# Turning the tie rule of a list scheduler round once all groups of work are under way, in a four-layer graph network kernel

## Chip, cores and metric

The kernel runs on one core of a Trainium2 chip. The metric is the device time of one execution in microseconds (us). Engines are called PE (TensorE), ACT (ScalarE), DVE (VectorE), POOL (GpSimd) and SP (SyncE, which here only starts transfers).

## What is computed

128 graphs of 128 nodes with 128 features each go through four pre-norm attention layers. With `h = relu(layernorm(x))` ahead of each layer and `x = x + layer(h)` after it, the layers are, per graph:

```
layer 0: D[i,j] = |h[i]-h[j]|;  s = leaky(batchnorm(D @ W1.T)) @ W2;  A = softmax(masked s)
         y = leaky(batchnorm(A @ h @ Wg.T + bg));  out = [h, y] @ Wt.T + bt
layer 1: 8-head graph attention (leaky(f1[i]+f2[j]), masked softmax), elu, one more single head, elu
layer 2: single-head graph attention, elu
layer 3: 8 bilinear edge types, score chosen by the edge's type, softmax, value and output projections
```

The two batch norms of layer 0 run over all 128 graphs, so nothing after them can begin before the last graph has been seen.

## The kernel before

The program falls into three stages. **Stage A** builds the pairwise differences of every graph, multiplies them with W1 and gathers their mean and variance (`nodes` and `pairs`, with four `block`s to a graph; 160 pieces of work). **Stage B** normalises them, forms the scores, the softmax and y (`graph_scores`, `score_table`, `edges`, `attention`, then `y_norm`, `edge_types` and `first_inputs`; 179 pieces of work). **Stage C** does the rest of layer 0 and layers 1 to 3 for four graphs at a time (`group`, 32 of them, numbered 0 to 31 here). Stage C exists twice in the program, for adjacency values of only 0 and 1 and for any; a branch on `types` picks one, and with these inputs the first runs.

Within a stage no order of instructions is written out. Each piece of work is a generator that yields steps: an engine, a planned duration, the buffers that the step takes and those that it frees; a `fork` starts a side chain (a head, an edge type), and a `join` waits for it. The function `in_order` (line 54) plays all generators that are under way against each other on a planned clock. At each turn it works out for every chain when its next step could begin: not before its engine is free, its input is ready and its buffers are to be had. It emits the step that could begin first. What it emits is the program order of each engine, which nothing reorders afterwards (`manual_schedule`). At most `most` pieces of work are under way at a time: 6 in stage A, 10 in stage B, 6 in stage C. When one ends, the next begins.

Many chains usually wait for one busy engine, and then they could all begin at the same moment, when that engine comes free. So the order among equals decides much of the schedule. It is `(begin, c["age"], k)` in line 132: first the earliest beginning, then the age (the number of the piece of work; side chains have their parent's), then the place in the list. A lower age is an older piece of work. Apart from that, some buffers are kept for the oldest piece under way (`kept`): in stage C one PSUM bank `ps`, six tiles `t`, three tiles `w` and one `v`.

Steps of a group in stage C that are named below, with their lines:

- `yl` (L1136, L425), `po` of the first layer (L1142, L1145) and its sum `x` (L1150)
- the layer norm: statistics (L929, L931, L933) on DVE, `rs` (L936) on POOL, `nb` (L939) on DVE, `h` (L943) on ACT, the transposes `pt` (L951) on PE, their copy `hTc` (L954) on ACT
- `pv` (L1165) and `pf` (L1174), the values and the attention vectors of the eight heads, and `f1d` (L1195)
- the heads: `z` (L1069, L959) on PE, `p` and `q` (L1078, L1079) on ACT, `p` (L963) on DVE, `pa` (L1092) on PE, `xh` (L1098, L1099) on DVE; four such steps to a group
- after the heads: `xc` (L1214, L1216), `ptx` (L1221), `xcT` (L1224), `ph` (L1234)
- two single heads: `z` (L1243 or L1269, L1271), exponentials (L974 or L971), `po` (L1007), `ri`, `xh` (L1014, L1016), `ex` (L986), `xo` (L997, L990)
- layer 3: `pd` (L1290), `pv` (L1311), `pp` (L1104), `tt` (L1107), `ps` (L1111), the choice (L1318), exponentials (L1321, L1322), `p` (L1324), `po` (L1007), the sum `x` (L1336) and its store (L1337)

PSUM in stage C is four banks of `ps` and two double banks of `pz`; the heads' `z`, `ptx`, `ph` and `po` all take `pz`.

In stage B a score table is made of eight graphs: their score matmuls (L699), `us` (L718) on DVE, four transfers out (L728) and one in (L739) on POOL's queue, `u` (L781) on POOL, and then two `attention`s: `pl` (L788, L790, L791), `mx` and `e` (L796, L798), `pt` (L810), `py` (L817), `yt` (L820), and the store of `y` (L822). `edges` makes `negm` (L754) and `pz` (L762).

Of the kernel before, what the change touches and what calls it, by code (L numbers as in the profile page):

```python
# [51 lines left out]


def in_order(makers, most, room, kept):

    free_at = dict.fromkeys(AFTER, 0.0)
    slots = {kind: [0.0] * n for kind, n in room.items()}
    chains, events = [], {}
    started = under_way = 0
    now = 0.0

    def step(c, at):

        nonlocal under_way
        c["ready"] = at  # L70
        while True:
            said = next(c["gen"], None)
            if said is None:
                chains.remove(c)
                up = c["parent"]
                if up is None:
                    under_way -= 1
                    return
                up["open"] -= 1
                up["last"] = max(up["last"], at)  # L80
                if up["joins"] and not up["open"]:
                    up["joins"] = False
                    step(up, max(up["ready"], up["last"]))
                return
            if said[0] == "fork":
                c["open"] += 1
                step(chain(said[1], c), at)
            elif said[0] == "join":
                if c["open"]:
                    c["joins"] = True  # L90
                    return
            elif said[0] == "free":
                for kind in said[1].split():
                    slots[kind].append(at)
            elif said[0] == "wait":
                c["ready"] = at = at + said[1]
            elif said[0] == "done":
                events[said[1]] = at
            elif said[0] == "after":
                c["after"] = said[1]  # L100
            else:
                c["next"] = said
                return

    def chain(gen, parent):
        c = {"gen": gen, "parent": parent, "age": parent["age"] if parent else started, "open": 0,
             "last": 0.0, "joins": False, "next": None, "ready": 0.0, "after": None}
        chains.append(c)
        return c

    while started < len(makers) or chains:
        while started < len(makers) and under_way < most:
            under_way += 1
            c = chain(makers[started](), None)
            started += 1
            step(c, now)
        best = None
        oldest = min(c["age"] for c in chains)
        for k, c in enumerate(chains):
            if c["next"] is None or (c["after"] is not None and c["after"] not in events):  # L120
                continue
            engine, _, takes, _ = c["next"]
            begin = max(free_at[engine], c["ready"], events.get(c["after"], 0.0))
            takes = takes.split()
            for kind in set(takes):
                spare = 0 if c["age"] == oldest else kept.get(kind, 0)
                at = sorted(slots[kind])
                m = takes.count(kind)
                begin = max(begin, at[m - 1]) if len(at) >= m + spare else None
                if begin is None:  # L130
                    break
            if begin is not None and (best is None or (begin, c["age"], k) < best[0]):
                best = (begin, c["age"], k), c
        (now, _, _), c = best
        engine, work, takes, frees = c["next"]
        for kind in takes.split():
            slots[kind].remove(min(slots[kind]))
        free_at[engine] = now + work
        end = now + work + AFTER[engine]
        for kind in frees.split():  # L140
            slots[kind].append(end)
        c["next"] = c["after"] = None
        step(c, end)
# [16 lines left out]
def kernel(ctx: ExitStack, tc: tile.TileContext, x, adj, w, out):  # L160
# [269 lines left out]
    with tc.tile_pool(name="h_pool", bufs=1) as h_pool, tc.tile_pool(name="pairs", bufs=B_V) as b_v:  # L430
# [10 lines left out]
        with tc.tile_pool(name="a2", bufs=2) as a2, tc.tile_pool(  # L441
# [148 lines left out]
            with tc.manual_schedule(engines=ORDERED):  # L590
                in_order(makers, A_UNDER_WAY, {"d": A_D, "ph": 3, "v": B_V} | two, A_KEPT)
# [32 lines left out]
        with tc.tile_pool(name="b2", bufs=2) as b2p, tc.tile_pool(name="b_s", bufs=2, space=PSUM) as b_s, tc.tile_pool(  # L624
# [256 lines left out]
            with tc.manual_schedule(engines=ORDERED):  # L881
                in_order(
                    makers, B_UNDER_WAY, {"v": B_V - KEEP, "r": B_R, "pb": 6, "u": 4} | two, {"pb": 2}
                )
# [5 lines left out]
    def layers(simple):  # L890

        with tc.tile_pool(name="c_in", bufs=3) as c_in, tc.tile_pool(
# [231 lines left out]
            def group(g):  # L1124
# [213 lines left out]

            load(1)
            in_order(  # L1340
                [partial(group, g) for g in range(NB // GC)], UNDER_WAY,
                {"ps": 4, "pz": 2, "t": C_T, "w": C_W, "vals": C_V, "f": C_V, "v": C_O, "mask": C_M},
# [46 lines left out]
```

## Times and profile before

| what | us |
|---|---|
| three runs | 3172.33, 3160.60, 3168.47 |
| their median | 3168.47 |
| the profiled execution | 3172.22 |
| its span in the trace | 3170.4 |
| stage A, until its last statistics (L581, L521) | 0 to about 1248.4 |
| stage B, until `y_bi` (L417) | about 1248.5 to 2059.9 |
| stage C | 2060.0 to 3170.4 |
| of it, from the last group's `yl` on | 2975.7 to 3170.4 |

| engine | busy us | share of the span |
|---|---|---|
| PE | 2876.5 | 91% |
| DVE | 2655.7 | 84% |
| ACT | 2627.2 | 83% |
| POOL | 1494.6 | 47% |

The page cuts the span into 40 slices and shows for each the busy tenths of each engine and the clock that PE was granted (`PEclk`, in tenths of full speed). The trace gives the same for any window, and, for any window, each engine's instructions in order of time with the idle time ahead of each and what ended it.

### The profile page before, as it was taken

To read this page: it belongs to the slowest core of one execution; us is meant where nothing else is said; L and a number is where in the kernel's file an instruction comes from. 1 tells how busy PE (TensorE), PEld (TensorE's weight loads), DVE (VectorE), ACT (ScalarE), POOL (GpSimd) and SP (SyncE) were. 2 spreads that over 40 slices of the span, in tenths; PEclk is the share of its full clock that TensorE was granted. 3 is DMA by queue.
4 is the path that set the end of the run, shared out by engine and by line. 5 is a ranking of instruction groups with operands and counts; after the bars stand their busy time and mean duration, and the time that the engine had idled before them with its cause. 6 is when DMAs were issued, how large, how long until landed. Compare 5 with 4: busy or idle time off the path is not lost. (4 is left out here: it accounts for less than half of the span.)

```text
span 3170.4 us, 47435 instructions
## 1 busy us (share of the span) xinstructions
PE 2876.5 (91%) x17577; PEld 1601.7 (51%) x17577; DVE 2655.7 (84%) x4730; ACT 2627.2 (83%) x3050; POOL 1494.6 (47%) x953
## 2 busy tenths in 40 slices
PE   6999999999999998878888888689999999999996
PEld 3444433433343443233333333377787777877774
DVE  6999999999999999768777686577878878888864
ACT  4999999999999998878788787467878778877774
POOL 5999999999999996011111111122222122212211
PEclk9999999999999999989999898889999999999997
DMA  3555555555655551999999999321111111111000
GB/s 118 238 237 247 238 244 224 241 234 224 250 227 234 243 219 37 415 405 382 404 404 392 392 393 394 124 67 31 47 34 43 43 34 34 54 31 41 11 11 12
DMA packets 150723, 606.53 MB, mean 191 GB/s; under 512 B 15634, under 2 KB 99027, under 8 KB 119763
## 3 DMA queue, kind: packets, MB, share of 16 engines
q1 hardware_dynamic: 140242, 569.86, 45.6%
q0 software_dynamic: 10240, 33.53, 2.9%
q8 instruction: 143, 2.34, 0.3%
q14 instruction: 98, 0.79, 0.1%
HBM read 322.74 MB, written 280.61 MB: 190 GB/s over the span
## 5 line engine op out<-in xcount | busy, mean ns | idle before, releaser
L549 POOL TENSOR_TENSOR d<-he 128x2016 f32<-128x2016 f32 (+1 forms) x288 | 1021.6, 3572 | 63.9 <-PE ph L566 59.4
L566 PE MATMUL ph<-d,w1T 128*64 128x512 f32 (+1 forms) x4096 | 927.2, 595 | 34.6 <-DVE d L546 16.9
L552 ACT ACTIVATE d<-d 128x2016 f32<-128x2016 f32 (+1 forms) x352 | 676.7, 1926 | 13.3 <-POOL d L549 13.2
L581 DVE BATCH_NORM_STATS2 six<-v 128x6 f32<-128x512 f32 (+1 forms) x1024 | 624.0, 669 | 4.4 <-ACT v L576 4.3
L566 PEld LDWEIGHTS ph<-d,w1T 128*64 128x64 f32 x4096 | 308.0, 136 | 543.9 <-issue 397.3
L576 ACT COPY v<-ph 128x1024 f32<-128x1024 f32 (+1 forms) x512 | 510.9, 1032 | 28.9 <-PE ph L566 25.9
L546 DVE TENSOR_TENSOR d<-he,pt 128x2048 f32<-128x2048 f32 (+1 forms) x224 | 505.1, 2256 | 2.3 <-PE ph L566 2.3
L936 POOL TENSOR_TENSOR rs<-ve,nhalf 128x4 f32<-128x4 f32 x96 | 120.1, 1251 | 778.8 <-DVE ve L933 561.4
L425 DVE SCALAR_TENSOR_TENSOR v<-v 128x1528 f32<-128x1528 f32 x256 | 433.9, 1741 | 33.2 <-ACT v L654 32.6
L654 ACT ACTIVATE v<-v,h_bi,h_sc 128x1528 f32<-128x1528 f32 x256 | 412.9, 1660 | 6.9 <-DVE h_bi L417 6.9
L699 PE MATMUL sc<-v,w_slide 128*32 128x512 f32 (+1 forms) x1536 | 322.3, 601 | 17.2 <-DVE v L425 16.9
L1092 PE MATMUL pa<-vals,p 128*128 128x99 f32 (+2 forms) x2048 | 256.8, 281 | 13.8 <-DVE p L963 10.7
L1092 PEld LDWEIGHTS pa<-vals,p 128*128 128x128 f32 x2048 | 251.4, 199 | 32.4 <-DVE p L963 15.0
L699 PE MATMUL sc<-v,w_line 128*32 128x504 f32 x512 | 260.8, 591 | 0.0
L699 PE MATMUL sc<-r,w_relu 128*32 128x504 f32 x512 | 258.6, 587 | 0.0
L963 DVE SCALAR_TENSOR_TENSOR p<-p,q 128x1024 f32<-128x1024 f32 (+1 forms) x192 | 206.5, 1082 | 49.9 <-ACT q L1079 25.2
L566 PE MATMUL ph<-both,us 128*64 128x512 bf16 x1920 | 236.6, 379 | 0.0
L566 PEld LDWEIGHTS <-us 128*64 128x64 bf16 x1920 | 124.4, 110 | 147.6 <-issue 91.8
L1078 ACT ACTIVATE p<-z 128x1024 f32<-128x1024 f32 x128 | 133.2, 1040 | 36.6 <-PE z L959 36.2
L661 ACT ACTIVATE r<-v,h_bi,h_sc 128x1008 f32<-128x1008 f32 x128 | 157.1, 1227 | 0.0
L800 ACT ACTIVATE e<-e 128x512 f32<-128x512 f32 x32 | 20.2, 630 | 153.9 <-DVE e L798 153.9
L788 PE MATMUL pl<-u,ident 128*128 128x512 f32 x64 | 49.8, 870 | 106.6 <-POOL u L781 106.6
(255 smaller groups left out, 4564.4 us busy)
## 6 DMA issues: line engine op xcount, KB each, us to landing
v<-v SPq DMA_DIRECT2D x240, 2032.0 KB, 8.9
xg<-in_x SPq DMA_DIRECT2D x64, 256.0 KB, 3.0
ht<-h SPq DMA_DIRECT2D x64, 256.0 KB, 6.1
u<-s POOLq DMA_DIRECT2D x16, 768.0 KB, 11.8
h<-he SPq DMA_DIRECT2D x32, 256.0 KB, 2.6
adj<-in_adj SPq DMA_DIRECT2D x32, 256.0 KB, 2.9
adj<-in_adj POOLq DMA_DIRECT2D x32, 256.0 KB, 8.3
y<-yt POOLq DMA_DIRECT2D x32, 256.0 KB, 6.3
```

The source lines that it names most:

```text
L425: engine.scalar_tensor_tensor(out, v, slope, v, ALU.mult, ALU.max)
L546: nc.vector.tensor_tensor(dv, later, own, ALU.max if larger else ALU.subtract)
L549: nc.gpsimd.tensor_tensor(dv, later, own, ALU.subtract)
L552: nc.scalar.activation(d[:, 0 : 4 * n], d[:, 0 : 4 * n], AF.Abs)
L566: nc.tensor.matmul(ph[64 * a : 64 * a + 64, t, 0:n], wt, x_, start=part == 0, stop=not larger or part == 3,)
L576: nc.scalar.copy(v.rearrange("p (t e) -> p t e", t=2), ph[:, :, 0:n])
L581: nc.vector.bn_stats(made["six"][:, 2 * q + t, :], v[:, t * n : t * n + n])
L654: nc.scalar.activation(part, part, AF.Identity, bias=h_bi, scale=h_sc)
L661: nc.scalar.activation(made["r"][:, 0:n], part, AF.Relu, bias=h_bi, scale=h_sc)
L699: nc.tensor.matmul(sc[rows, 0:n], wz[:, 31 - k : 63 - k], z, start=begins and q < NQ, stop=ends and q != NQ - 1, tile_position=(0, rows.st ...
L963: nc.vector.scalar_tensor_tensor(p, p, FLOOR, q, ALU.max, ALU.max)
L1092: nc.tensor.matmul(pa_all[:, h * (DH + 1) : h * (DH + 1) + n], p[:, h, :], vals_all[:, e : e + n], start=True, stop=True,)
```

## The change

```
-            if begin is not None and (best is None or (begin, c["age"], k) < best[0]):
-                best = (begin, c["age"], k), c
+            rank = begin, c["age"] if started < len(makers) else -c["age"], k
+            if begin is not None and (best is None or rank < best[0]):
+                best = rank, c
         (now, _, _), c = best
```

`started` counts the pieces of work that have begun and `len(makers)` those of the stage. While some are still to begin, the rule is the old one: among steps that could begin at the same moment, that of the oldest piece goes first. From the moment when the last one has begun, that of the youngest goes first. What is kept for the oldest piece stays as it was, and so do the planned durations and the buffers. `in_order` is called once in stage A, once in stage B and once in each copy of stage C, so the rule turns round in all of them: in A for the last six pieces (the graphs 122 to 127), in B for the last ten, in C for the last six groups. The two blank lines that the diff adds at the top of the function shift the lines of the changed kernel by two, and its later ones by three.

## Prediction

> **What bounds the kernel now.** I read first the slices of the page, because the new rule acts only where the last pieces of each stage are under way.
>
> ```profile
> PE   6999999999999998878888888689999999999996
> DVE  6999999999999999768777686577878878888864
> ACT  4999999999999998878788787467878778877774
> PEclk9999999999999999989999898889999999999997
> ```
>
> Stage A (the first fifteen slices) keeps three engines full. Stage C, from slice 27 on, is bound by PE; in the last slice everything falls and PE's clock falls too. The window table tells how long that drain is. Columns: window, length, then busy us (instructions) of PE, PEld, DVE, ACT, POOL, then the clock, the DMA share and GB/s. The first window starts where the last group begins and the two rules part, the third where the last group is alone; the last is stage C before that.
>
> ```profile
> 2976.00:3080.00 104.00, 98.01 (x743) 79.55 (x744) 82.26 (x232) 81.00 (x142) 16.34 (x24) 1.00 0.03 9
> 3080.00:3148.50 68.50, 49.21 (x268) 37.96 (x266) 35.82 (x100) 35.41 (x70) 8.52 (x12) 0.81 0.04 12
> 3148.50:3170.40 21.90, 11.43 (x42) 7.22 (x42) 2.95 (x5) 5.40 (x10) 1.31 (x2) 0.66 0.06 16
> 2100.00:2976.00 876.00, 832.55 (x6212) 682.36 (x6211) 700.47 (x1868) 687.47 (x1214) 192.87 (x260) 0.98 0.13 36
> ```
>
> In the plateau PE is busy 832.55/876 = 95%. In 3080 to 3148.5 it is idle for 19.3 of 68.5 us, and no other engine is full either: there are too few chains left. PE's waits there are the chain of one group, layer norm and softmax:
>
> ```profile
> PE pt L951 <- ACT h L943: 5.9, 1, 5.9
> PE po L1007 <- DVE p L963: 4.2, 1, 4.2
> PE po L1007 <- DVE p L1324: 3.6, 2, 2.8
> PE pa L1092 <- DVE p L963: 3.3, 1, 3.3
> ```
>
> The same matmuls also take longer there. From PE's timeline (start, us), one head step in the dense part and two after a pause:
>
> ```profile
> 3051.00 1.92 PE L1092 MATMUL pa<-vals,p 128*128 128x99 f32 x16
> ...
> 3088.30 3.40 PE L1092 MATMUL pa<-vals,p 128*128 128x99 f32 x16
> ...
> 3098.80 3.51 PE L1092 MATMUL pa<-vals,p 128*128 128x99 f32 x16 [3.29 <-DVE p L963]
> ```
>
> Stage B ends differently. Its last eight graphs' scores release a long chain through transfers, and on PE work of the table before stands ahead of them:
>
> ```profile
> 2008.84 1.16 PE L762 MATMUL pz<-wgT,ht 128*128 128x128 f32 x8
> 2009.84 1.04 PE L810 MATMUL pt<-ident,e 128*128 128x128 f32 x8
> 2011.41 2.05 PE L817 MATMUL py<-eT,zg 128*128 128x128 f32 x16 [0.54 <-ACT eT L813]
> 2013.39 0.62 PE L699 MATMUL sc<-v,w_slide 128*32 128x512 f32 x3
> ```
>
> **What the Trainium skill says.** "TensorE: Matmul & The Clock Gate", Part 1, says that PE's clock is halved by default and released after some 3.4 us of sustained work, and halved again after an idle window of that length. The trace agrees: clock 1.00 in the dense window, 0.81 and 0.66 in the drain, and 1.92 us against 3.40 and 3.51 for the same step. "PSUM — Partial Sum Buffer", Engine vs sequencer instructions, says that ACT, DVE and POOL take their queues strictly in order and that matmuls stay in program order. The waits above agree: each PE wait holds all that follows. "Perfetto Trace Analysis", Identifying the Most-Contended Engine, warns that matmul busy time is no measure of distance to the peak. So I use it only to compare windows of the same work.
>
> **The change part by part.** Listing the new program's order beside the old one, each engine has the same instructions in the same number; only three stretches are permuted. Nothing is added or removed; every cost is one of position.
>
> *Stage C.* The listing says that the old rule finishes the groups in the order 26, 27, 28, 29, 30, 31, one after the other, and the last 22 us belong to 31 alone. The new rule lets 29 and 31 do their heads first, leaves 26, 27 and 28 standing, and then all six end close together: 31, 29, 30, 27, 26, 28. On PE, between group 28's last weighted sum before layer 3 and its last transposes, now stand two `ps` steps, a `pv`, a `ps`, two `pp`, two `ps` and two `po`. At dense durations (`ps` x16, that is two steps, 1.95; `pv` 1.05; `pp` x4, two steps, 1.88; `po` 1.05) this is 1.95 + 1.05 + 0.98 + 1.88 + 1.95 + 2.10 = 9.9 us. In the same place group 31 left PE idle for 5.9 us. So the gap is filled, and 28's transposes are held a little.
>
> What stays alone is the last group from its transposes to the end: 21.9 us before, and I take 21.9 after. (The copy `hTc` of 28 stands behind 26's exponentials on ACT, about 1.3 us; the transposes meet a warm clock and save about 1.)
>
> Ahead of that stood 3148.5 - 2976 = 172.5 us with 98.01 + 49.21 = 147.2 us of PE work. From this goes the slow clock. Long against dense durations in 3080 to 3148.5: two `pa` 3.4, two `pd` (2.07 and 2.08 against 1.05) 2.0, `pv` 0.6 and 0.9, `po` 0.3 and 1.0, `pt` 0.5 and 0.7, `ptx` 0.9, `pp` 0.4; sum 10.7. Work left: 136.5 us. How densely it runs I can't read. From above it is bounded by the plateau's 95% (143.7 us), from below by little better than the old rule's 147.2/172.5 = 85% over the same stretch: 87%, with the slow clock half gone, 142/0.87 = 163. I take 90%, since no fresh groups come: 151.7 us. Gain 172.5 - 151.7 = **21 us** (9 to 29). ACT cannot forbid it: 81.0 + 35.4 = 116 us of work, DVE 118, both below 144. Nor can loads: the last group's `adf` and bias were computed by 2963, before the rules part.
>
> *Stage B.* PE's order becomes: scores, `pl`, scores, `pl`, scores, one `pz`, the last scores; the other `pz`, both `pt` and both `py` come after. What leaves the path of the last scores is 2008.84 to 2013.39, that is 4.55 us. DVE must follow: two `negm`, the second `mx` and `e` and both normalisations move behind the last leaky steps or between them. By my count those end near 2010.5, while PE reaches the last scores at about 2013.4 and ends them at 2017.0 rather than 2021.5. Then the chain goes as before (`us`, transfers out, transfer in, `u`, `pl`). The store of `y` of one attention now stands between the transfers out and the one in on POOL's queue: its `yt` comes about 5 us after the scores' end, and the transfer in was issued 6.6 us after it (2021.5 to 2028.15), so it fits by about a microsecond. Half a microsecond for contention with that store and the loads of stage C, which move with it: gain **4 us** (1 to 4.5).
>
> *Stage A.* In 1189 to 1236 ACT is busy 47.00 of 47.00, and then until its last copy ends at 1246.6 it waits 0.4 us. The order of its last six graphs can't do the same work faster. It can stall: 155's last block is now the last on POOL, and its ACT, PE, ACT and DVE steps follow one another. Loss **1 us** (0 to 4).
>
> Sum: 21 + 4 - 1 = 24 us. The profiled execution took 3172.2, 3.7 above the median of the runs; taken off the median, 3168.5 - 24 = 3144.5 us.
>
> **The rivals.**
>
> *The gain is mostly lost to the buffers.* The heads of 29, 31, 30 and 28 lie close together and share two `pz` banks with every `ptx`, `ph` and `po`; and the buffers kept for the oldest group, 26, stand idle while that group waits. For it: PE's longest total waits in the plateau are `z` for ACT's `q` (6.6 us) and `pa` for `p` (6.5 us), the heads' own turn. Against: a head costs PE about 2.7 us and holds ACT 1.85, so two banks suffice. At 87% of 142 us C gains 9; with B 4 and A losing 3, the time is 3158.5.
>
> *Slower: lockstep.* Six groups in the same section want the same engine at the same moment, and in order one late step holds the rest. The planner prices `f1d` at 0.8 us where it takes about 1.5, so its idea of who is ready drifts. In the old drain PE idles 28% (19.3 of 68.5). If the new tail ran so throughout, 147.2/0.72 = 204 us, 32 more than 172.5; less B, and A 1 worse: 3197. It costs more than it brings from the point where PE idles over 15% ahead of the last stage. Against it: the planner's other durations are close to the trace's (`pa` 1.7 against 1.76 to 1.9, a head's `p` and `q` 1.85 against 1.83), and the list above shows different sections side by side.
>
> *The full gain.* Plateau density and a full clock: 29 us in C, 4.5 in B, none lost in A: 3135.
>
> That nothing happens is no rival: the order of instructions does change.
>
> **How the numbers follow.** Forecast about 3144.5 (own range 3137 to 3153): 0.60. Full gain, 3135: 0.10. Lost to buffers, 3158.5: 0.20. Lockstep, 3197: 0.10. Half a per cent of 3168.5, about what a measurement can tell from no change, is 16 us, so faster begins below 3152.6: 0.70 faster, 0.20 the same, 0.10 slower. The range leaves out the lockstep and a few at the fast end: 3131 to 3163.
>
> **What would show it.** Right: in the last 22 us one group alone, ahead of that PE at about 90% and clock 1.0 up to some 25 us from the end, `pa` under 2 us throughout; the wait of 5.9 us for `h` gone; stage C from `y_bi` to the end about 1090 us against 1110.5. In B the last `us` begins about 4.5 us earlier, relative to the last `u` transfer before it. In A the last statistics end within 4 us of 1248.4. Wrong: waits of PE for ACT's `q` or for DVE's `p` spread over the tail, or two idle groups at the end rather than one; or an `us` that comes earlier while `u` does not.

## The result and the profile after

| | us |
|---|---|
| before, five runs by then | median 3160.60 (3153.99 to 3172.33) |
| changed, five runs | median 3131.72 (3127.06 to 3136.13) |
| ratio changed to before | 0.9899, 95% interval 0.9872 to 0.9925 |
| forecast | 3144.5 from 3168.5, ratio 0.9924 |

So the kernel became faster, by 1.0% (24 to 40 us of 3160.6). The changed kernel, measured once more with other kernels, gave 0.9920 (0.9897 to 0.9943). The forecast had the direction and the places right. Its time is 12.8 us above the one measured, and 7.9 of these come from where it started: the three runs known then have a median of 3168.5, all five one of 3160.6. Its ratio, 0.9924, lies at the edge of the first interval and inside the second. That the gain was larger than the forecast is therefore shown by the traces, and not by the run times alone.

To see where the time went, I cut both traces at the same six instructions: in stage A a row of four `six` (statistics of a tile, DVE), up to which both kernels have the same order, and `mv_s`, which reads the finished statistics; then the starts of stage B's last two `us`, the end of `y_bi`, the start of the last group's `yl`.

| stretch, us | before | changed | difference |
|---|---|---|---|
| start to the four `six` | 1186.27 | 1184.12 | -2.15 |
| to A's `mv_s` (the statistics are complete) | 62.19 | 64.28 | +2.09 |
| to the start of the second-last `us` | 732.8 | 730.2 | -2.6 |
| to the start of the last `us` | 40.39 | 36.04 | -4.35 |
| to the end of `y_bi` | 38.3 | 37.3 | -1.0 |
| to the last group's `yl` | 915.8 | 912.9 | -2.9 |
| from there to the end of the span | 194.7 | 165.1 | -29.6 |

The first, third and sixth stretch hold the same instructions in the same order in both kernels. Their differences are the spread of one execution against another, and the profiled execution of before was as slow as the slowest of its runs. The fifth holds a part of B's new order, but its 1.0 us is within the spread, too (36.7 to 38.3 us in the traces of all kernels below). What the rule moved is in the second, the fourth and the last: 2.1 us lost, 4.35 and 29.6 won, 31.9 us in this pair of traces. That is 1.0% of 3160.6.

The loss in stage A is easily missed, because `mv_s` comes at nearly the same time in both traces (1248.46 and 1248.40): the changed one happened to be 2.15 us ahead until then. Counted from the four `six`, it is plain. Before:

```profile
1186.27 2.45 DVE L581 BATCH_NORM_STATS2 six<-v 128x6 f32<-128x512 f32 x4
1248.46 0.28 DVE L379 TENSOR_REDUCE mv_s<-st 128x1 f32<-128x128 f32 x1
```

And changed:

```profile
1184.12 2.44 DVE L584 BATCH_NORM_STATS2 six<-v 128x6 f32<-128x512 f32 x4
1248.40 0.29 DVE L382 TENSOR_REDUCE mv_s<-st 128x1 f32<-128x128 f32 x1
```

From the start of the four `six` to that of the stage's last `six` it is 61.06 to 61.08 us in the four traces with A's old order (before and E1 to E3 below) and 63.16 to 63.19 in the ten with the new one. In this stretch ACT waits for PE's products 1.6 us longer (total, times, longest; before, then changed):

```profile
ACT v L576 <- PE ph L566: 0.4, 1, 0.4
ACT v L579 <- PE ph L569: 2.0, 3, 1.1
```

The slices of the changed kernel's page, against those shown for before. In the last slice DVE and ACT have 6 tenths instead of 4, PE 7 instead of 6, and the clock 9 instead of 7:

```profile
PE   6999999999999999787988888879999999999997
DVE  6999999999999999776877877667787787787886
ACT  4999999999999998887877878657777877787786
PEclk8999999999999999898999999989999999999999
```

The tail, cut at the last group's final transposes rather than at fixed times. The first two lines are the changed kernel's trace, with columns as in the prediction.

```profile
2965.10:3110.67 145.57, 137.35 (x993) 111.59 (x1002) 115.18 (x324) 115.61 (x213) 25.67 (x38) 0.99 0.03 8
3110.67:3129.90 19.23, 8.59 (x52) 5.97 (x50) 6.69 (x12) 4.96 (x9) 0.40 (x2) 0.84 0.17 50
```

The same cut in the trace of before:

```profile
2976.00:3148.48 172.48, 147.20 (x1010) 117.50 (x1010) 118.08 (x331) 116.39 (x212) 24.85 (x36) 0.93 0.03 10
3148.48:3170.40 21.92, 11.45 (x42) 7.24 (x42) 2.95 (x5) 5.42 (x10) 1.31 (x2) 0.66 0.06 16
```

Ahead of the last transposes PE works 137.35 us instead of 147.20, because the clock is 0.99 rather than 0.93, and it does so in 145.57 us, which is 94.4% of the time rather than 85.3%. The changed kernel's second trace (E9 below) has 144.2 and 19.3 us for the two parts. The solo at the end (from the last transposes `pt` on) is shorter by 2.7 us. The changed kernel's timeline:

```profile
3110.67 0.60 PE L954 MATMUL pt<-ident,h 128*128 128x128 f32 x4
3111.95 1.12 PE L1293 MATMUL pd<-hTc,kwT 128*128 128x512 f32 x2 [0.68 <-ACT hTc L957]
...
3114.22 1.06 PE L1314 MATMUL pv<-vpw,hTc 128*128 128x128 f32 x8
3115.11 1.88 PE L1107 MATMUL pp<-hTc,aq 128*128 128x512 f32 x4
```

And before, for the same four steps:

```profile
3148.48 1.63 PE L951 MATMUL pt<-ident,h 128*128 128x128 f32 x4 [5.91 <-ACT h L943]
3150.78 2.07 PE L1290 MATMUL pd<-hTc,kwT 128*128 128x512 f32 x2 [0.68 <-ACT hTc L954]
3152.65 1.91 PE L1311 MATMUL pv<-vpw,hTc 128*128 128x128 f32 x8
3154.36 3.19 PE L1104 MATMUL pp<-hTc,aq 128*128 128x512 f32 x4
```

About 1.0 us of it is won at `pt`, from whose start to that of `pd` it is now 1.28 us instead of 2.30. Before, the transposes follow ACT, which makes `h` for one of the four graphs after another; now `h` is ready. The clock has little part in this: in E3's trace they take 1.48 us in the same place, waiting for `h` in the same way, at a clock of 1.00. The other 1.7 us go with the clock, 0.84 in the solo instead of 0.66: from the start of `pd` to the end of `pp` it is 5.04 us instead of 6.77, although a `po` of another group now stands between `pd` and `pv`. After `pp` the solo is as long as before (12.9 us).

PE's waits over the whole tail, changed (total, times, longest). The waits for `h` and for the heads' `p` are gone or below a microsecond; what is left longest, 2.8 us, is the very last softmax, which took 2.8 before, too.

```profile
PE po L1010 <- DVE p L1327: 5.4, 4, 2.8
PE po L1010 <- DVE p L966: 1.4, 2, 0.9
```

In stage B the last `us` of the changed kernel starts 36.04 us after the one before it:

```profile
1978.58 1.52 DVE L721 TENSOR_SCALAR us<-sc,b_rows 64x512 f32<-64x512 f32 x2 [0.94 <-PE sc L702]
2014.62 1.53 DVE L721 TENSOR_SCALAR us<-sc,b_rows 64x512 f32<-64x512 f32 x2 [3.81 <-PE sc L702]
```

Before it was 40.39:

```profile
1981.23 1.52 DVE L718 TENSOR_SCALAR us<-sc,b_rows 64x512 f32<-64x512 f32 x2 [0.94 <-PE sc L699]
2021.62 1.52 DVE L718 TENSOR_SCALAR us<-sc,b_rows 64x512 f32<-64x512 f32 x2 [4.06 <-PE sc L699]
```

POOL's queue after it, changed. The store of `y` stands between the transfers out and the one in, and the one in is issued 6.66 us after the start of `us`, where before it was 6.53 (2021.62 to 2028.15). So it fitted.

```profile
2015.66 2.31 POOL L731 DMA_DIRECT2D s<-us  x4 [16.70 <-DVE us L721]
2019.45 0.59 POOL L825 DMA_DIRECT2D y<-yt  x1 [1.48 <-ACT yt L823]
2021.28 0.90 POOL L742 DMA_DIRECT2D u<-s  x1 [1.24 <-PE py L820]
```

### The profile page after: what moved, and what is told of

It is laid out like the page before. It is cut to its first block, busy times and chain, and to the rows that moved or that the text cites. A ratio compares the mean times of both kernels' runs of the same rounds, so it can differ in the third digit from the quotient of the medians.

```text
span 3129.9 us, 47376 instructions
## 1 busy us (share of the span) xinstructions
PE 2852.8 (91%) x17526; PEld 1588.3 (51%) x17577; DVE 2656.4 (85%) x4730; ACT 2626.3 (84%) x3050; POOL 1494.6 (48%) x953
## 5 line engine op out<-in xcount | busy, mean ns | idle before, releaser
L579 ACT COPY v<-ph 128x1008 f32<-128x1008 f32 (+1 forms) x512 | 509.6, 1028 | 30.7 <-PE ph L569 27.9
L702 PEld LDWEIGHTS sc<-v,w_slide 128*32 128x32 f32 x1536 | 65.1, 109 | 160.1 <-DVE v L428 83.3
```

The costliest lines, as they stand in the source:

```text
L579: nc.scalar.copy(v.rearrange("p (t e) -> p t e", t=2), ph[:, :, 0:n])
L702: nc.tensor.matmul(sc[rows, 0:n], wz[:, 31 - k : 63 - k], z, start=begins and q < NQ, stop=ends and q != NQ - 1, tile_position=(0, rows.st ...
```

## The experiments

All times are ratios to the kernel before on the same chip, with 95% intervals. "Tail" is the span from the start of the last group's `yl`; "C" is from `y_bi` to the end. Traces of one order spread: the tail of the changed kernel's order in C was 165.1, 163.4 and (E1) 167.4 us, that of before's order 194.7 and (E2) 194.6. Differences under about 4 us between kernels are therefore not told apart.

**E1 and E2: the stages apart.** The rule turned round in C alone, and in B alone.

```
-            rank = begin, c["age"] if started < len(makers) else -c["age"], k
+            rank = begin, c["age"] if started < len(makers) or len(makers) not in (32,) else -c["age"], k   # E1
+            rank = begin, c["age"] if started < len(makers) or len(makers) not in (179,) else -c["age"], k  # E2
```

> The rule turned round in stage C alone; stages A and B as before. My theory now: nearly all of the gain is made in C's own tail and stands by itself. From the last group's yl to the end about 165 us as in the changed kernel (194.7 before), ratio to before about 0.990 to 0.992. In B the time between the starts of the last two us (39.4 us before, 35.0 changed) is 39.4 again. Rival: C gains only because B hands over its loads and engines earlier; then the tail of C is over 175 us and the ratio 0.995 or more.

> The rule turned round in stage B alone. My theory: the last us starts 35.0 us after the one before it instead of 39.4, and the rest of B's chain is as long as before, so 4 to 5 us are gained: ratio about 0.9985. C's tail 194 to 195 us as before. Rival: the earlier us is eaten by the transfers, which then meet other traffic; y_bi comes as late as before, ratio 1.000.

E1: 0.9926 (0.9907 to 0.9944), a little less gain than expected, tail 167.4, `us` to `us` 40.39. E2: 0.9988 (0.9976 to 1.0001), tail 194.6, `us` to `us` 36.04, and `y_bi` 37.0 us after the last `us`. (The 39.4 and 35.0 in the expectation were counted from the store that follows the earlier `us`; from start to start they are 40.39 and 36.04, and the difference is the same 4.35.) Within the spread the stages are independent: C gives what it gives without B, and B's 4.35 us are not eaten. From the last `us` to `y_bi` all fourteen traces have 36.7 to 38.3 us, with the old order of B as with the new. E2's interval touches 1.000, so by run times alone B's gain is not shown; by the traces, where the stretch repeats to 0.02 us in all eleven with the new order, it is. A was not run by itself; its loss of 2.1 us is read from the traces.

**E3: the clock alone.** The order of before, with PE kept busy in three pauses of the last group.

```
+            def filled(to, fill, n):
+                for _ in range(n if fill is not None else 0):
+                    nc.tensor.matmul(to, ident_far, fill, start=True, stop=True)
...
                 pt = psum("pt")
+                filled(pt, fill, 24)
...
-                po = by_graph(psum2("po"))
+                po_all = psum2("po")
+                filled(po_all[:, 0, :], fill, 18)
+                po = by_graph(po_all)
...
+                if i == 3 and last:
+                    filled(pa_all, mask, 12)
```

> The order of before, and group 31 alone gets useless bf16 matmuls of 128x512 in three of PE's pauses, into banks that the next real matmuls overwrite: 12 ahead of its last head's pa, 18 ahead of its first single head's po, 24 ahead of its last transposes. Nothing of the result changes. Theory that the slow clock after pauses is a third of the gain: pa, pd, pv, pp and pt after these pauses take their dense durations (1.8, 1.1, 1.1, 1.9, 0.6) and the tail of C shortens by 6 to 11 us, ratio 0.997. Rival: the long durations are only how the trace models matmuls, or the waits alone count: the tail stays within 2 us of 194.7, or grows by what the filling delays.

Measured 0.9984 (0.9974 to 0.9995) where 0.997 was expected, tail 188.7: 6.0 us less than before, the low end of what was expected. In its trace the steps after the first filled pause are dense, where before they took 3.51, 1.09 and 2.07 us:

```profile
3095.95 2.54 PE L960 MATMUL pa<-mask,ident_far 128*128 128x512 bf16 x11
3099.18 1.97 PE L1101 MATMUL pa<-vals,p 128*128 128x99 f32 x16 [0.70 <-DVE p L968]
3100.99 0.63 PE L952 MATMUL pt<-ident,h 128*128 128x128 f32 x4
3102.30 1.13 PE L1300 MATMUL pd<-hTc,kwT 128*128 128x512 f32 x2 [0.67 <-ACT hTc L955]
```

So the long durations are real time and come from the pause, and useless work removes them. It did not do so everywhere: after the third filled pause the steps were slow again (`pd` 1.38, `pv` 1.92, `pp` 2.52 us, clock 0.68), against the expectation. So of the 29.6 us about 6 were had in this way, and more could perhaps be had. The clock's whole part, the order being as before, can't be more than the PE work that vanished from the tail, 158.66 - 145.94 = 12.7 us, so more than half of the gain is the waiting itself.

**E4: is it the youngest that must go first, or only that groups live late?** Least planned work done first, in steps of 30 planned us.

```
+            turned = started == len(makers)
+            first = (c["age"], 0) if not turned else (spent[c["age"]] // 30, -c["age"]) if level else (-c["age"], 0)
+            rank = begin, first, k
...
+        spent[c["age"]] += work
```

> As the changed kernel in A and B; in C, once all groups are under way, the one with the least planned work done goes first, in steps of 30 planned us, youngest first among equals. If what counts is that many groups live until late, whichever they are, the tail of C is again 162 to 168 us and the ratio 0.989 to 0.991. If the strict order youngest first is what counts, it is clearly worse, over 172 us. If levelling them more closely is better still, under 162 us.

Measured 0.9896 (0.9880 to 0.9912), tail 164.3, PE busy 146.98 us of it: as the changed kernel. Strict order of age is not needed.

**E5, E6 and E7: when the rule turns.** Only when at most four groups, or three, are under way; and two groups earlier.

```
+            turned = started == len(makers) and (len(makers) != 32 or under_way <= 4)   # E5; 3 in E6
+            rank = begin, -c["age"] if turned else c["age"], k
...
+            left = len(makers) - started - (2 if len(makers) == 32 else 0)              # E7
+            rank = begin, c["age"] if left > 0 else -c["age"], k
```

> As the changed kernel, but in stage C the rule turns round only when no more than four groups are under way, so 26 and 27 still end early, in the old way. Theory: the tail lasts as long as PE has too few chains, so fewer groups alive late give less, but four are still enough to fill most pauses: tail from the last yl 168 to 175 us (165.1 with six, 194.7 with none). Rival: the gain hangs on letting 29 and 31 do their heads at once; then it is mostly gone here, tail over 182 us.

> As before, with the turn only when three groups or fewer are under way. They still end one after the other (29, 30, 31), but closer. Theory: three chains cannot fill the pauses of one another fully: tail 176 to 188 us. Rival, that only the last group's solo matters: tail as long as with four or six.

> As the changed kernel, but in stage C the rule turns round two groups earlier, when two are still to begin. If six late groups already fill PE, there is nothing more to gain: stage C as a whole 1074 to 1082 us (1077.9 changed, 1110.5 before). If starving the old ones earlier ties up buffers, C is longer than 1085.

E5: 0.9932 (0.9910 to 0.9955), tail 181.8. E6: 0.9936 (0.9912 to 0.9959), tail 180.4. E7: 0.9944 (0.9927 to 0.9960), C 1092.4. E6 lies in its range, but it is as long as E5, which should have been 168 to 175: from three late groups to four nothing was won. E5 also comes within 0.2 us of its rival's mark of 182 (that 29 and 31 must do their heads at once), so it doesn't speak against that one. E7 lost nearly half of C's gain where I expected none lost. The traces show where the time goes. In E5 the late groups arrive in one section together. Three of them have their first single head side by side there. Two groups' transposes wait as one for the layer norms of both, and the third `po` before that for DVE; the clock drops too (2.09 us for a `po` of 1.06 to 1.14):

```profile
3082.77 2.09 PE L1011 MATMUL po<-h,p 128*128 128x131 f32 x8 [3.51 <-DVE p L967]
3088.31 3.17 PE L955 MATMUL pt<-ident,hv 128*128 128x128 f32 x8 [3.45 <-ACT hv L947]
```

ACT has both norms at that moment, eight instructions in one row:

```profile
3087.76 3.19 ACT L947 ACTIVATE hv<-xo,nb,rs 128x128 f32<-128x128 f32 x8 [1.30 <-DVE nb L943]
```

This is the lockstep of the prediction's second rival, in a kernel that I had not expected it in. E7 has it at the end. The starved groups are finished before, 30 and 31 come last and side by side, and PE waits for both at once, twice; in its last 47 us PE works 27.3:

```profile
3103.32 3.17 PE L955 MATMUL pt<-ident,hv 128*128 128x128 f32 x8 [6.72 <-ACT hv L947]
...
3120.57 1.63 PE L955 MATMUL pt<-ident,h 128*128 128x128 f32 x4 [4.50 <-ACT h L947]
```

E7's C is also above the 1085 us that were to tell of tied-up buffers, but these long waits are for layer norms.

So I mended the theory: PE is filled when many groups live late *and* stand in different sections. This is a reading of the traces; how much of the lost gain is lockstep and how much the smaller number of late groups, these three runs don't separate.

**E8: the kept buffers.** Nothing kept for the oldest piece once all are under way.

```
-                spare = 0 if c["age"] == oldest else kept.get(kind, 0)
+                spare = 0 if c["age"] == oldest or started == len(makers) else kept.get(kind, 0)
```

> As the changed kernel, but nothing is kept for the oldest piece once all are under way. The rival of the prediction said that buffers kept for a waiting oldest group cost time: then the tail is 3 us or more shorter than 165.1. My theory: PE is 94 per cent busy there anyway, so the tail is 163 to 167 us.

Measured 0.9888 (0.9871 to 0.9906), tail 168.0, just above the range. Not told apart from the changed kernel, and in any case not shorter: the buffers kept for the oldest cost nothing that shows. The other half of that rival, the heads' sharing of two `pz` banks, no run changes; in the changed kernel's trace PE's listed waits ahead of the heads' `z` and `pa` come to 1.4 us in the whole tail.

**E9 to E12: the mended theory, and the best version.** The changed kernel again; E4 and E8 together; the rule turned one group earlier (E7's edit with 1 for 2); E4's edit with 40 for 30.

> The changed kernel once more, beside the next three on the same chip. Ratio to before 0.989 to 0.992; tail of C from the last yl 164 to 168 us (165.1 in its first trace).

> Level rule of before (least planned work done first in C's tail, steps of 30 us) and nothing kept for the oldest in the tail, the two that came out lowest put together. Theory: PE is 94 per cent busy ahead of the last group's end in either, so they don't add up: tail 162 to 167 us, ratio 0.988 to 0.991. If keeping and levelling each take something of their own, the tail is under 161 us.

> The rule turned one group earlier in C. By the planned order no more than two groups live for the last 9 us of PE work and no more than three for the last 17 (changed kernel 5 and 10, turned two earlier 20 and 25, before 20 and 44). If the number of groups that live late decides, stage C as a whole lies between: 1079 to 1088 us. If turning early is bad in itself, it is near the 1092 of the kernel turned two earlier.

> The level rule with steps of 40 planned us rather than 30: groups end at other places, but again all late (no more than three for the last 6 us of PE work). Number of live groups decides: tail 162 to 168 us. If groups in the same section hold one another up, as in the kernel turned at four, the tail is 170 us or more and PE shows pauses of over 3 us before the last 25 us.

E9: 0.9920 (0.9897 to 0.9943), tail 163.4. E10: 0.9905 (0.9883 to 0.9927), tail 168.3, 1.3 above its range. E11: 0.9917 (0.9893 to 0.9941), C 1078.5, 0.5 below what the count of late groups gave, so that turning one group earlier lost nothing. E12: 0.9956 (0.9942 to 0.9969), tail 182.3. E12 tells most. At least as many groups live late as in E4 (three or fewer are left for the last 12.6 us before PE's end in its trace, for the last 16.3 in E4's), and it is 18 us longer. So the number of late groups does not decide alone. PE works 8.5 us longer than in E4 (155.5 against 147.0, at a clock of 0.94 against 0.98) and idles 9.4 us more (26.7 against 17.3). Its pauses are short (none above 2.9 us, against the over 3 that I had expected), but they are many.

Is it lockstep? E12 puts one kind of work of all groups first and then the next kind; on POOL, whose part in stage C is mainly the layer norms' `rs`, that shows as a gap of 53 us without any norm. But E4 has such a gap of 45 us and the changed kernel one of 34, so the gap alone doesn't tell the good orders from this one. That E12's groups stand in the same section, and lose by it, fits the mended theory and is not shown: no run moves the sections and nothing else.

No version is shown to beat the changed kernel. E4, E8, E10 and E11 have ratios of 0.9888 to 0.9917, all within the intervals of its two measurements.

## Why the prediction was too small

The mechanism held: the pauses of the drain were filled with work of other groups, and the clock stayed up. What failed are two terms of the sum for stage C, "I take 90%" for how densely PE works ahead of the last solo, where 94.4% was measured, and "I take 21.9 after" for the solo, where 19.23 us were measured. Point by point, by its own steps:

- **The order moves in three stretches and nothing is added: right.** Instruction counts per engine in the tail are the same but for missing matmul records (DVE 336, ACT 221, PE loads 1051 in both).
- **Stage A, a loss of 1 us (0 to 4): right in kind, 2.1 us measured.** ACT does wait there, as the prediction feared, 2.0 us instead of 0.4.
- **Stage B, 4.55 us off the path and 4 us gained: right.** The trace has 4.35 from `us` to `us`. The half microsecond for contention was mostly not needed; the store of `y` fitted between the transfers.
- **Stage C, the steps that fill the gap of 5.9 us: right.** The listed steps stand ahead of the last transposes and take 10.1 us (3100.55 to 3110.67), against the 9.9 forecast.
- **Stage C, PE work left 136.5 us once the slow clock is gone: right.** Measured 137.35.
- **"I take 90%, since no fresh groups come": wrong, and the larger part of the miss.** Measured 94.4%, next to the plateau's 95%. 136.5/0.90 = 151.7 against the 145.57 measured is 6.1 us. In this tail the lack of fresh groups cost next to nothing. I had the plateau's figure as the upper bound and no reading for going below it.
- **"What stays alone ... I take 21.9 after": wrong by 2.7 us.** I had set a gain of about 1 us at the transposes against a delay of `hTc` by 26's exponentials. The gain came (1.0 us, because `h` was ready rather than because of the clock). The delay did not (PE waited 0.68 us for `hTc`, as before). And `pd`, `pv` and `pp` gained 1.7 us by the clock: I had worked out such dense durations for the part ahead and did not carry them into the solo.
- **Sum.** 6.1 + 2.7 = 8.8 us is the difference between the 20.8 (rounded to 21) that I forecast for C and the 29.6 in the pair of traces. With A and B, 24 us were forecast and 31.9 measured. The case "the full gain" (29 in C, 4.5 in B, none lost in A) describes what happened but for A's 2.1 us, and I gave it 0.10.
- **The rivals.** Buffers: E8 speaks against the kept ones. Lockstep: not in this kernel, whose tail has no wait above 2.8 us, but real: the traces of E5 and E7 show it. They and E12, where it is not shown, have tails (E7: C) 14 to 18 us longer than the changed kernel or E4, and so has E6, where three groups end one after the other. None of them is slower than before, so nothing here comes near the rival's price of 32 us over the old drain.

What stays open: why the planner's order with E4's steps of 30 runs as well as the changed kernel and with steps of 40 does not. That follows from planned durations and ties and was not traced further. How much of the 29.6 us the clock makes up lies between the 6 us of E3 and the 12.7 us of PE work that vanished.

## What to carry to other kernels

In a list scheduler like this one many choices are ties on the busy engine, so the tie rule makes much of the schedule. Oldest first was fine while new work kept coming (PE 95% busy), but it ended in a queue of lone chains; turning it round for the last pieces, so that they end together, gave 1%. Look at how the late pieces stand to one another, too: E12, with as many of them, kept about half of that gain. When costing such a change, ask for a reading before going below the plateau's density for the filled stretch (here the plateau's 95% would have been nearly right), and take the clock into the last solo as well. And compare two traces from the last instruction up to which their order is the same: counted from the start, the spread of 2.15 us hid the loss in stage A.

## What the runs showed of the hardware

Filling PE's pauses with useless bf16 matmuls shortened the real matmuls after them: a head's `pa` 1.97 us against 3.51, `pt` 0.63 against 1.09, `pd` 1.13 against 2.07, and the kernel by 0.16% (0.05 to 0.26). I had taken the slow clock as a thing to subtract; that some of it can be bought off with idle time that is there anyway I had only half expected.

The prediction speaks of an idle window of some 3.4 us after which the clock is halved. The pauses of 4.16 and 5.91 us before fit that, but shorter ones were followed by slow steps as well: 2.49 us before (a `pa` of 3.40 us at 3088.30, clock 0.56), and 1.09 and 1.32 us close together in E12 (a `pa` of 3.30 us at 3015.85, clock 0.58). So in these traces the length of one pause is not enough to tell whether the clock will fall.
